# A mixture-of-experts stage on one core: experts ordered by a rough choice, buffers freed in pairs, weight halves loaded first, the last unit in two PSUM banks

## The chip, the core and the metric

One core of a Trainium2 chip runs the whole program. Its engines are TensorE (PE in the profile, with PEld for its weight loads), VectorE (DVE), ScalarE (ACT), GpSimd (POOL) and the sync engine (SP), which here issues the loads from HBM. The metric is the time of one execution on the device, in microseconds.

## The reference

Input `x` is 128 tokens of width 512. Three residual blocks follow one another: a cross-attention to 12,544 context tokens, a self-attention with 16 heads of width 128, and a mixture of experts. Only the third is touched by the change; this is what it computes (`x` there is the layernorm of the running sum, n = 128):

```
logits = x @ gate_w.T;  scores = sigmoid(logits);  sc = scores + gate_bias      # 32 experts
group_scores = sum of the two largest sc in each of 4 groups of 8 experts
gidx = the 2 best groups;  tmp = where(group chosen, sc, 0)
topk_idx = the 4 largest of tmp;  topk_w = scores[topk_idx] / their sum * 2
y   = sum over chosen experts of topk_w * ( silu(x @ w1[e]) * (x @ w3[e]) ) @ w2[e]   # 512 -> 256 -> 512
out = y + ( silu(x @ shared_gate) * (x @ shared_up) ) @ shared_down                   # 512 -> 512 -> 512
```

Ties in either choice go to the lower index.

## The kernel before

The two attention blocks take about the first 960 us of the profiled execution and are the same in both kernels. The expert block then runs as follows (all in `fast_block`; every tensor is fp32, so each matmul of the program is two instructions in the trace).

**Gating.** A layernorm, four transposes and one small product give the scores `sc` (DVE, through the helper `vec`, L1996: every small DVE step of this block has that line). The exact choice follows in fifteen dependent DVE steps: it ranks the groups with ties resolved (`gt`, `eq`, `rank`, `gsel`), masks the scores (`kept_`), takes the eight largest (`t8`), and selects the top four with ties resolved (`over_`, `n_over`, `equal`, `run`, `sel`). The helper `pin` keeps instructions in the order in which the code writes them.

**Order of the experts.** Experts 0 to 5 are "fixed": their weights are loaded during the self-attention and every token is put through them. The other 26 are sorted by how many tokens chose them. `sort_experts` counts with two small matmuls (`counts`, L2151 and L2152, from `sel`), then makes sort keys, each expert's place and the one-hot matrix `hot` on DVE. `find_loads` turns this into expert numbers with one matmul (`index`, L2169) and a DVE step; SP reads the numbers into registers and then issues the loads (`load_piece`, L1850). `gates` computes the gate values from `sel`.

**Units.** Fifteen units follow each other in the order `ffffnffntnwwntn`: `f` is a fixed expert; `t` one of the two most-chosen experts, put to all 128 tokens; `w` two experts of up to 64 tokens each; `n` four experts of up to 32 tokens each. The experts of one `w` or `n` unit are its lanes: they use separate columns of TensorE side by side. A unit has four steps. `unit_up` (L2075) multiplies by w1 and w3 in four chunks of 128 rows, all lanes of a chunk before the next chunk. `unit_act` computes silu(gate part) * up part on ACT and DVE. `unit_turn` (L2102) transposes on TensorE. `unit_down` multiplies by w2 (L2116 `y` for `w` and `n` units, L2062 `acc` for the others). For `w` and `n` units `unit_combine` (L2062) adds the rows back to their tokens. The main loop is software-pipelined: turn of unit u, up of u+1, combine of u-1, down of u.

**Loads.** Each of the 26 sorted experts comes in three pieces of 512 KB: piece 0 holds chunks 0 and 1 of w1 and w3, piece 1 holds chunks 2 and 3, piece 2 holds w2. That makes 78 loads, issued by SP in one fixed order. Before, a unit's pieces come as lane 0 piece 0, lane 0 piece 1, lane 1 piece 0, and so on, and then all pieces 2. A piece goes to the first buffer in a list `free`. `release` puts the buffers of a unit back after its up and after its down step; the load that takes a buffer waits until TensorE has read it. In program order each load also waits for the load eight before it.

**Shared expert.** Its six 512 KB buffers are filled during the self-attention. It runs inside the loop at units 5 (`shared_gate`), 6 (`shared_up`, then `check_sums`, whose small matmul `n_far`, L2315, waits for a DVE chain), 7 (`shared_turn`) and 11 (`shared_down`). All six buffers go back to `free` after `shared_down`.

Of the kernel before, what the change touches and what calls it, by code (L numbers as in the profile page):

```python
# [10 lines left out]
AF = mybir.ActivationFunctionType  # L11
ALU = mybir.AluOpType
# [758 lines left out]
def fast_block(ctx: ExitStack, tc: tile.TileContext, a: dict, out: bass.AP, amiss: bass.AP):  # L771
# [115 lines left out]
    def row(tag, name, shape=(P, D)):  # L887
        return xc.tile(list(shape), FP, tag=tag, name=name)
# [1044 lines left out]
    shared, shared_parts = {}, []  # L1933
    for nm, where in (
        ("shared_gate", homes[6][:2]),
        ("shared_up", [homes[6][2], homes[7][0]]),
        ("shared_down", homes[7][1:]),
    ):
        shared[nm] = [where[c // 2][:, c % 2 * D : c % 2 * D + D] for c in range(NC)]
        shared_parts += where  # L1940
# [34 lines left out]
    loads = []  # L1975
    for kind, lanes, _ in units:
        if kind != "all":
            loads += [(i, k) for i, _, _ in lanes for k in range(2)] + [(i, 2) for i, _, _ in lanes]

    h3 = rowp.tile([P, D], FP, tag="h", name="h3")  # L1980
    layernorm(h3, x2, "x2", pin)
    warm = spare("warm_h3")
# [23 lines left out]
    gs = row("gs", "gs", (P, G))  # L2006
    vec("tensor_tensor", gs, m8[:, :, 0], m8[:, :, 1], ALU.add)


    other = gs.unsqueeze(1).to_broadcast([P, G, G])  # L2010
    own = gs.unsqueeze(2).to_broadcast([P, G, G])
    gt = row("gt", "gt", (P, G, G))
    vec("tensor_tensor", gt, other, own, ALU.is_gt)
    eq = row("eq", "eq", (P, G, G))
    vec("tensor_tensor", eq, other, own, ALU.is_equal)
    vec("tensor_tensor", eq, eq, before, ALU.mult)
    vec("tensor_tensor", gt, gt, eq, ALU.add)
    rank = row("rank", "rank", (P, G))
    vec("tensor_reduce", rank, gt, AX.X, ALU.add)
    gsel = row("gsel", "gsel", (P, G))  # L2020
    vec("tensor_scalar", gsel, rank, float(TG), None, ALU.is_lt)
    kept_ = row("kept_", "kept_", (P, E))
    vec(
        "tensor_tensor",
        kept_.rearrange("p (g e) -> p g e", g=G),
        sc.rearrange("p (g e) -> p g e", g=G),
        gsel.unsqueeze(2).to_broadcast([P, G, E // G]),
        ALU.mult,
    )

    t8 = row("t8", "t8", (P, 8))
    vec("max", t8, kept_)
    bound = t8[:, TOPK - 1 : TOPK]
    over_ = row("over_", "over_", (P, E))
    vec("tensor_scalar", over_, kept_, bound, None, ALU.is_gt)
    n_over = row("n_over", "n_over", (P, 1))
    vec("tensor_reduce", n_over, over_, AX.X, ALU.add)
    equal = row("equal", "equal", (P, E))  # L2040
    vec("tensor_scalar", equal, kept_, bound, None, ALU.is_equal)
    run = row("run", "run", (P, E))
    vec("tensor_tensor_scan", run, ones[:, :E], equal, 0.0, ALU.mult, ALU.add)
    sel = row("sel", "sel", (P, E))
    vec("tensor_scalar", sel, run, n_over, float(TOPK), ALU.add, ALU.is_le)
    vec("tensor_tensor", sel, sel, equal, ALU.mult)
    vec("tensor_tensor", sel, sel, over_, ALU.add)


    acc = ps_o.tile([P, D], FP, tag="o", name="acc")  # L2050
# [76 lines left out]
    def unit_combine(u):  # L2127
        if units[u][0] == "some":
            k = units[u][2]
            add_to_acc(back[:, k * P : (k + 1) * P], outs[u % 2], u == len(units) - 1)  # L2130

    index_of = {}

    def release(u, pieces):
# [12 lines left out]
    def sort_experts():  # L2147

        n = SORTED
        ct = bank("counts", (P, 128))  # L2150
        pin(nc.tensor.matmul(ct[:n, :n], lhsT=ones[:, :n], rhs=sel[:, FIXED:], start=True, stop=True))  # L2151
        pin(nc.tensor.matmul(ct[:n, n : n + 1], lhsT=sel[:, FIXED:], rhs=ones[:, 0:1], start=True, stop=True))  # L2152

        keys = row("keys", "keys", (P, SORTED + 1))
        vec("scalar_tensor_tensor", keys[:n, :n], ct[:n, :n], float(E), nat[:n, :n], ALU.mult, ALU.subtract)
        vec("scalar_tensor_tensor", keys[:n, n:], ct[:n, n : n + 1], float(E), nat_col[:n], ALU.mult, ALU.subtract)
        more = row("more", "more", (P, SORTED))
        vec("tensor_scalar", more[:n], keys[:n, :n], keys[:n, n:], None, ALU.is_gt)
        place = row("place", "place", (P, 1))
        vec("tensor_reduce", place[:n], more[:n], AX.X, ALU.add)  # L2160
        vec("tensor_scalar", place[:n], place[:n], 1.0, None, ALU.add)
        hot = row("hot", "hot", (P, SORTED))
        vec("tensor_scalar", hot[:n], nat[:n, :n], place[:n], None, ALU.is_equal)
        return hot[:n]

    def find_loads(hot):
        n = SORTED
        ix = bank("index", (P, 128))
        pin(nc.tensor.matmul(ix[0:1, :n], lhsT=nat_col[:n], rhs=hot, start=True, stop=True))  # L2169
        index = small.tile([1, SORTED], mybir.dt.int32, tag="index", name="index")  # L2170
        vec("tensor_scalar", index, ix[0:1, :n], float(FIXED - 1), float(E - 1), ALU.add, ALU.min)
        order = []
# [20 lines left out]
            load_more()  # L2193

    def gates():
        vec("tensor_tensor", gate, sel, prob, ALU.mult)
        wsum = row("wsum", "wsum", (P, 1))
        vec("tensor_reduce", wsum, gate, AX.X, ALU.add)
        vec("tensor_scalar", wsum, wsum, 1e-20, None, ALU.add)
        winv = row("winv", "winv", (P, 1))  # L2200
        vec("reciprocal", winv, wsum)
        vec("tensor_scalar", gate, gate, winv, ROUTE_SCALE, ALU.mult, ALU.mult)
# [125 lines left out]
    sorted_gates_b(hot)  # L2328
# [20 lines left out]
    for u in range(3, n):  # L2349
# [19 lines left out]
    pin(nc.sync.dma_start(out=out, in_=res))  # L2369
# [80 lines left out]
```

## Time and profile before

| | us |
|---|---|
| median of three timed runs | 1094.71 (1092.88 to 1095.63) |
| time of the profiled execution | 1091.79 |
| its span, first to last instruction | 1090.1 |
| mean granted TensorE clock | 0.997 |
| expert block, from the first unit's matmul to the last instruction of the output | 966.8 to 1084.6 |
| PE busy over the whole span | 1064.8 (98%) |

The page shares are averages over three blocks with different limits, so the answers that matter here are those cut to the time after 966 us: busy time and DMA rate by stretch, who waited for whom, the chain that ended last, and the rows in order of time. In the DMA rows the time of an issue is when SP issued it, and the landing comes later.

### The profile page before, as it was taken

The numbers are of one execution on the slowest core, as the hardware profiler recorded it, in microseconds if no ns is written. First come the engines' busy times: TensorE is split into PE (matmuls) and PEld (weight loads), VectorE is DVE, ScalarE is ACT, GpSimd is POOL, SyncE is SP. The second block draws the span as 40 slices with busy tenths as digits, with TensorE's granted clock in tenths as the row PEclk, the third lists the DMA queues.
The fourth block names the chain that finished last, engine by engine and source line by source line (L and its number), as shares of the span: only waits on it lengthen the run. The fifth ranks groups of instructions, "written<-read, shape, count | busy, mean of one in ns | idle before, by whom it ended". The sixth has DMA issues, their size and how long they took to land.

```text
span 1090.1 us, 23595 instructions
## 1 busy us (share of the span) xinstructions
PE 1064.8 (98%) x10464; PEld 844.3 (77%) x10464; DVE 545.6 (50%) x668; ACT 356.1 (33%) x438; POOL 691.0 (63%) x374
## 2 busy tenths in 40 slices
PE   8999999999999999999999999999999899999996
PEld 6778888888888888888888888888888669754332
DVE  3676864574445544455444554445544568441110
ACT  2353333333333333333333333333333324303111
POOL 2256886887878778787787888889888600000000
PEclk9999999999999999999999999999999999999999
DMA  9221021101111011110124201111010499519995
GB/s 307 90 79 41 2 88 40 41 1 40 40 40 41 2 40 40 40 41 2 40 82 165 59 2 40 40 40 40 1 41 1 141 390 368 174 72 413 384 414 234
DMA packets 43247, 113.17 MB, mean 104 GB/s; under 512 B 6720, under 2 KB 12032, under 8 KB 42112
## 3 DMA queue, kind: packets, MB, share of 16 engines
q1 hardware_dynamic: 43136, 111.57, 28.2%
q8 instruction: 84, 1.38, 0.5%
q14 instruction: 27, 0.22, 0.1%
HBM read 111.26 MB, written 0.29 MB: 102 GB/s over the span
## 4 chain that ended last, share of the span: by engine, by line
PE 89%; DVE 3%; DMA 3%; POOL 2%; ACT 1%; issue 1%; SPq 0%; DVEq 0%; ACTq 0%; POOLq 0%
PE kp L1078 27%; PE vp L1078 25%; PE sb L1162 10%; PE av_new L1268 8%; PE up L2075 4%; PE acc L2062 2%; PE ssq L1015 1%; PE qp L1759 1%; PE kp L1759 1%; PE yp L1917 1%; PE svp L1780 1%; PE vp L1230 1%; DMA h<-in_experts 1%; DMA wo<-in_experts 1%; DMA wv<-in_experts 1%; DVE p L1251 1%
## 5 line engine op out<-in xcount | busy, mean ns | idle before, releaser
L1426 POOL TENSOR_TENSOR ls<-ls,p 128x2048 f32<-128x2048 f32 x81 | 369.1, 4556 | 38.2 <-ACT p L1259 36.6
L1259 ACT ACTIVATE p<-p 128x2048 f32<-128x2048 f32 (+1 forms) x95 | 179.9, 1893 | 462.1 <-DVE p L1251 461.9
L1251 DVE SCALAR_TENSOR_TENSOR p<-sb,rinv,mb_new 128x2048 f32<-128x2048 f32 (+1 forms) x86 | 199.9, 2325 | 59.2 <-PE sb L1162 59.2
L1123 POOL TENSOR_TENSOR sq<-sq 128x512 f32<-128x512 f32 x96 | 96.2, 1002 | 33.1 <-ACT sq L1117 29.3
L1162 PE MATMUL sb<-qT_txt,kraw 32*128 32x128 f32 (+1 forms) x3040 | 111.5, 283 | 1.5 <-DVE p L1251 1.5
L1162 PEld LDWEIGHTS sb<-qT_txt,kraw 32*128 32x128 f32 (+1 forms) x3040 | 93.4, 186 | 19.6 <-issue 17.1
L1078 PE MATMUL kp<-xs,w_k_w 128*128 128x256 f32 x384 | 95.4, 392 | 0.0
L1078 PE MATMUL kp<-ctx,w_k_w 128*128 128x256 f32 x384 | 93.3, 386 | 0.0
L1078 PE MATMUL kp<-xs,kt 128*128 128x256 f32 x384 | 92.7, 385 | 0.1
L1268 PE MATMUL av_new<-p,v 128*32 128x128 f32 (+1 forms) x2720 | 92.5, 276 | 0.0
L1078 PE MATMUL vp<-vt,xs 128*128 128x256 f32 x384 | 91.1, 380 | 1.1 <-ACT kraw L1106 1.1
L1078 PE MATMUL vp<-w_v_w,xs 128*128 128x256 f32 x384 | 90.9, 380 | 0.0
L1078 PE MATMUL vp<-w_v_w,ctx 128*128 128x256 f32 x384 | 90.8, 380 | 0.0
L818 POOL TENSOR_TENSOR rinv<-ms,neghalf 128x2 f32<-128x2 f32 (+4 forms) x51 | 39.6, 778 | 71.2 <-DVE ms L1025 71.2
L1078 PEld LDWEIGHTS kp<-xs,kt 128*128 128x128 f32 x384 | 73.6, 193 | 11.4 <-POOL wk L1426 0.4
L1078 PEld LDWEIGHTS kp<-xs,w_k_w 128*128 128x128 f32 x384 | 69.3, 190 | 16.3 <-issue 8.9
L1078 PEld LDWEIGHTS vp<-vt,xs 128*128 128x128 f32 x384 | 72.8, 190 | 11.4 <-ACT kraw L1106 1.6
L1078 PEld LDWEIGHTS kp<-ctx,w_k_w 128*128 128x128 f32 x384 | 70.9, 190 | 13.7 <-issue 5.3
L1078 PEld LDWEIGHTS vp<-w_v_w,xs 128*128 128x128 f32 x384 | 72.9, 190 | 10.0
L1078 PEld LDWEIGHTS vp<-w_v_w,ctx 128*128 128x128 f32 x384 | 72.9, 190 | 9.8
L1268 PEld LDWEIGHTS av_new<-p,v 128*32 128x32 f32 (+1 forms) x2720 | 69.6, 110 | 11.2 <-issue 1.2
L818 POOL TENSOR_TENSOR rs_x<-ve_x,neghalf 128x1 f32<-128x1 f32 x3 | 1.7, 551 | 101.2 <-DVE ve_x L826 101.2
(441 smaller groups left out, 1470.4 us busy)
## 6 DMA issues: line engine op xcount, KB each, us to landing
ctx<-in_ctxT SPq DMA_DIRECT2D x23, 1024.0 KB, 4.9
wo<-in_experts SPq DMA_DIRECT2D x20, 512.0 KB, 9.9
wo<-in_wo_codes SPq DMA_DIRECT2D x8, 512.0 KB, 6.9
wq<-in_experts SPq DMA_DIRECT2D x8, 512.0 KB, 9.8
wk<-in_experts SPq DMA_DIRECT2D x8, 512.0 KB, 9.2
wv<-in_experts SPq DMA_DIRECT2D x8, 512.0 KB, 9.2
q<-in_experts SPq DMA_DIRECT2D x8, 512.0 KB, 9.4
f<-in_experts SPq DMA_DIRECT2D x8, 512.0 KB, 9.7
```

The costliest lines, as they stand in the source:

```text
L818: return nc.gpsimd.tensor_tensor(dst, src, neghalf[:m, :n], op=ALU.pow)
L1015: pin(nc.tensor.matmul(sp[:m, j : j + 1], lhsT=sq[b][:, 0, o : o + m], rhs=ones[:, 0:1], start=True, stop=True,))
L1078: pin(nc.tensor.matmul(t[:, h, :], lhsT=lhs, rhs=rhs, start=(first and h == 0 and c == 0), stop=(h == 1 and c == 1), skip_group_check=True,))
L1123: pin(nc.gpsimd.tensor_tensor(sq[b][:, :w, ks], sq[b][:, :w, ks], sq[b][:, w : 2 * w, ks], op=ALU.add))
L1162: pin(nc.tensor.matmul(s[:m, i, g * P : (g + 1) * P], lhsT=kraw[b][rows, g, o : o + m], rhs=qT[part][rows, g, :], start=True, stop=True,))
L1251: pin(nc.vector.scalar_tensor_tensor(p[:m, k : k + n], s[:m, k : k + n], rinv[:m, t : t + 1], m_bc[part][:m, k : k + n], ALU.mult, ALU.sub ...
L1259: pin(nc.scalar.activation(p[:m, k : k + n], p[:m, k : k + n], AF.Exp))
L1268: pin(nc.tensor.matmul(avp[part][i * XHD : (i + 1) * XHD, g, :], lhsT=vv[b][:m, t - tile0[b], hd * XHD : (hd + 1) * XHD], rhs=p[:m, i, g * ...
L1426: pin(nc.gpsimd.tensor_tensor(d, d, src, op=ALU.add))
L1759: pin(nc.tensor.matmul(pp[:, k, :], lhsT=w[:, c, k * SHD : (k + 1) * SHD], rhs=hT2[:, c, :], start=(c == 0), stop=(c == NC - 1),))
L2062: pin(nc.tensor.matmul(acc, lhsT=lhsT, rhs=rhs, start=(n_acc == 0), stop=last))
L2075: pin(nc.tensor.matmul(up[r : r + m, :], lhsT=lhsT, rhs=w13_of((kind != "all", i), c), start=(c == 0), stop=(c == NC - 1), skip_group_chec ...
```

## The change

1. **Rough choice.** The two best groups are found by a threshold (the second largest of four group scores, from an eight-wide maximum over the scores padded with -3e38), the scores of other groups are set to zero in the same step, and every score not below the fourth largest is marked (`rough`). This takes four DVE steps. `counts` reads `rough`. The fifteen steps of the exact choice become a generator, `choosing`: two steps are issued after the `counts` matmuls, two after the `index` matmul, the rest at the start of `gates`. A memset on POOL fills the padding ahead of the layernorm.
2. **Opening order.** Before: up of unit 0, one chunk of unit 1, sort, one chunk of unit 1, find loads, gates, two chunks of unit 1. After: three chunks of unit 0, sort, the last chunk of unit 0, find loads, gates, up of unit 1. In the sort, `place + 1` is folded into the comparison that makes `hot`.
3. **Halves first.** A unit's loads are all its pieces 0, then all pieces 1, then all pieces 2.
4. **Shared buffers by twos.** The two buffers of `shared_gate` and of `shared_up` go back to `free` as soon as each has been used.
5. **Last unit in two banks.** For the last unit the gate half and the up half (256 columns each) have a PSUM bank each, in the order gate 0, up 0, gate 1, up 1, then the combine of unit 12, then gate 2, gate 3, up 2, up 3. The sigmoid and the first product are issued after gate 3.

```diff
-            loads += [(i, k) for i, _, _ in lanes for k in range(2)] + [(i, 2) for i, _, _ in lanes]
+            loads += [(i, k) for k in range(3) for i, _, _ in lanes]
...
+    gs8 = row("gs8", "gs8", (P, 8))
+    pin(nc.gpsimd.memset(gs8, -3e38))
...
+    g8 = row("g8", "g8", (P, 8))
+    vec("max", g8, gs8)
+    rough = row("rough", "rough", (P, E))
+    vec("scalar_tensor_tensor", by_group(rough), gs.unsqueeze(2).to_broadcast([P, G, E // G]),
+        g8[:, TG - 1 : TG], by_group(sc), ALU.is_ge, ALU.mult)
     t8 = row("t8", "t8", (P, 8))
-    vec("max", t8, kept_)
+    vec("max", t8, rough)
+    vec("tensor_scalar", rough, rough, t8[:, TOPK - 1 : TOPK], None, ALU.is_ge)
...
+    def last_unit():
+        u = len(units) - 1
+        _, lanes, at_ = units[u]
+        up = [spare(f"up_{u}_{h}", (P, F)) for h in range(2)]
+        for h, c in [(0, 0), (1, 0), (0, 1), (1, 1), (0, 2), (0, 3), (1, 2), (1, 3)]:
+            if (h, c) == (0, 2):
+                unit_combine(u - 2)
+            for i, r, m in lanes:
+                pin(nc.tensor.matmul(up[h][r : r + m, :],
+                    lhsT=picked[c][:, at_ * P + r : at_ * P + r + m],
+                    rhs=w13_of((True, i), c)[:, h * F : (h + 1) * F],
+                    start=(c == 0), stop=(c == NC - 1), skip_group_check=True))
+            if (h, c) == (0, 3):
+                sig = held["sig"][:, u % 2, :]
+                pin(nc.scalar.activation(sig, up[0], AF.Sigmoid))
+                hg = held["hg"][:, u % 2, :]
+                pin(nc.vector.tensor_tensor(hg, up[0], sig, ALU.mult))
+        pin(nc.vector.tensor_tensor(hg, hg, up[1], ALU.mult))
...
-        vec("tensor_scalar", place[:n], place[:n], 1.0, None, ALU.add)
-        vec("tensor_scalar", hot[:n], nat[:n, :n], place[:n], None, ALU.is_equal)
+        vec("tensor_scalar", hot[:n], nat[:n, :n], -1.0, place[:n], ALU.add, ALU.is_equal)
...
     def gates():
+        for _ in choosing:
+            pass
...
         vec("tensor_tensor", ssig, ssig, sp[nm], ALU.mult)
+        free.extend(shared_parts[nm])
+        load_more()
...
-        free.extend(shared_parts)
+        free.extend(shared_parts["shared_down"])
...
-    unit_up(0)
-    unit_up(1, [0])
+    unit_up(0, [0, 1, 2])
     hot = sort_experts()
-    unit_up(1, [1])
+    unit_up(0, [3])
     find_loads(hot)
     gates()
-    unit_up(1, [2, 3])
+    unit_up(1)
     sorted_gates_a()
...
-        if u + 1 < n:
+        if u + 1 < n - 1:
             unit_up(u + 1)
             unit_act(u + 1)
-        unit_combine(u - 1)
+        elif u + 1 < n:
+            last_unit()
+        if u != n - 2:
+            unit_combine(u - 1)
         unit_down(u)
```

More of the change, by code (lines that the diff above doesn't have):

```diff
@@ L1932, in fast_block @@
     ao_halves = halves(ao.rearrange("p j b i -> p j (b i)"))
-    shared, shared_parts = {}, []
+    shared, shared_parts = {}, {}
     for nm, where in (
@@ L1939, in fast_block @@
         shared[nm] = [where[c // 2][:, c % 2 * D : c % 2 * D + D] for c in range(NC)]
-        shared_parts += where
+        shared_parts[nm] = where
         for h, t in enumerate(where):
@@ L2005, in fast_block @@
         vec("max", m8[:, g, :], sc[:, g * (E // G) : (g + 1) * (E // G)])
-    gs = row("gs", "gs", (P, G))
+    gs = gs8[:, :G]
     vec("tensor_tensor", gs, m8[:, :, 0], m8[:, :, 1], ALU.add)
[L2010 to L2022, printed above, removed]
-    vec(
[L2024 to L2027, printed above, removed]
+    by_group = lambda t: t.rearrange("p (g e) -> p g e", g=G)
+    g8 = row("g8", "g8", (P, 8))
+    vec("max", g8, gs8)
+    rough = row("rough", "rough", (P, E))
+    vec(
+        "scalar_tensor_tensor",
+        by_group(rough),
+        gs.unsqueeze(2).to_broadcast([P, G, E // G]),
+        g8[:, TG - 1 : TG],
+        by_group(sc),
+        ALU.is_ge,
         ALU.mult,
@@ L2033, in fast_block @@
     t8 = row("t8", "t8", (P, 8))
-    vec("max", t8, kept_)
[L2035 to L2043, printed above, removed]
@@ L2044, in fast_block, with choose @@
-    sel = row("sel", "sel", (P, E))
-    vec("tensor_scalar", sel, run, n_over, float(TOPK), ALU.add, ALU.is_le)
-    vec("tensor_tensor", sel, sel, equal, ALU.mult)
-    vec("tensor_tensor", sel, sel, over_, ALU.add)
+    vec("max", t8, rough)
+    vec("tensor_scalar", rough, rough, t8[:, TOPK - 1 : TOPK], None, ALU.is_ge)
+    sel = row("sel", "sel", (P, E))
+    def choose():
+        other = gs.unsqueeze(1).to_broadcast([P, G, G])
+        own = gs.unsqueeze(2).to_broadcast([P, G, G])
+        gt = row("gt", "gt", (P, G, G))
+        yield vec("tensor_tensor", gt, other, own, ALU.is_gt)
+        eq = row("eq", "eq", (P, G, G))
+        yield vec("tensor_tensor", eq, other, own, ALU.is_equal)
+        yield vec("tensor_tensor", eq, eq, before, ALU.mult)
+        yield vec("tensor_tensor", gt, gt, eq, ALU.add)
+        rank = row("rank", "rank", (P, G))
+        yield vec("tensor_reduce", rank, gt, AX.X, ALU.add)
+        kept_ = row("kept_", "kept_", (P, E))
+        gsel = row("gsel", "gsel", (P, G))
+        yield vec("tensor_scalar", gsel, rank, float(TG), None, ALU.is_lt)
+        yield vec(
+            "tensor_tensor",
+            by_group(kept_),
+            by_group(sc),
+            gsel.unsqueeze(2).to_broadcast([P, G, E // G]),
+            ALU.mult,
+        )
+        k8 = row("k8", "k8", (P, 8))
+        yield vec("max", k8, kept_)
+        bound = k8[:, TOPK - 1 : TOPK]
+        over_ = row("over_", "over_", (P, E))
+        yield vec("tensor_scalar", over_, kept_, bound, None, ALU.is_gt)
+        n_over = row("n_over", "n_over", (P, 1))
+        equal = row("equal", "equal", (P, E))
+        yield vec("tensor_scalar", equal, kept_, bound, None, ALU.is_equal)
+        yield vec("tensor_reduce", n_over, over_, AX.X, ALU.add)
+        run = row("run", "run", (P, E))
+        yield vec("tensor_tensor_scan", run, ones[:, :E], equal, 0.0, ALU.mult, ALU.add)
+        yield vec("tensor_scalar", sel, run, n_over, float(TOPK), ALU.add, ALU.is_le)
+        yield vec("tensor_tensor", sel, sel, equal, ALU.mult)
+        yield vec("tensor_tensor", sel, sel, over_, ALU.add)
@@ L2050, in fast_block @@
+    choosing = choose()
     acc = ps_o.tile([P, D], FP, tag="o", name="acc")
@@ L2130, in unit_combine @@
             add_to_acc(back[:, k * P : (k + 1) * P], outs[u % 2], u == len(units) - 1)
+    def last_unit():
[6 more added lines that the diff above has]
+            for i, r, m in lanes:
+                pin(nc.tensor.matmul(
+                    up[h][r : r + m, :],
+                    lhsT=picked[c][:, at_ * P + r : at_ * P + r + m],
+                    rhs=w13_of((True, i), c)[:, h * F : (h + 1) * F],
+                    start=(c == 0),
+                    stop=(c == NC - 1),
+                    skip_group_check=True,
+                ))
+            if (h, c) == (0, 3):
[4 more added lines that the diff above has]
+        pin(nc.vector.tensor_tensor(hg, hg, up[1], ALU.mult))
     index_of = {}
@@ L2150, in sort_experts @@
         ct = bank("counts", (P, 128))
-        pin(nc.tensor.matmul(ct[:n, :n], lhsT=ones[:, :n], rhs=sel[:, FIXED:], start=True, stop=True))
-        pin(nc.tensor.matmul(ct[:n, n : n + 1], lhsT=sel[:, FIXED:], rhs=ones[:, 0:1], start=True, stop=True))
+        pin(nc.tensor.matmul(ct[:n, :n], lhsT=ones[:, :n], rhs=rough[:, FIXED:], start=True, stop=True))
+        pin(nc.tensor.matmul(ct[:n, n : n + 1], lhsT=rough[:, FIXED:], rhs=ones[:, 0:1], start=True, stop=True))
+        next(choosing)
+        next(choosing)
         keys = row("keys", "keys", (P, SORTED + 1))
@@ L2169, in find_loads @@
         pin(nc.tensor.matmul(ix[0:1, :n], lhsT=nat_col[:n], rhs=hot, start=True, stop=True))
+        next(choosing)
+        next(choosing)
         index = small.tile([1, SORTED], mybir.dt.int32, tag="index", name="index")
```

## Prediction

> **What bounds the kernel now.** I read four answers on the expert block, in this order: busy time by stretch, the waits of TensorE, the chain that ended last, and the rows at the two ends. Busy time by stretch:
>
> ```profile
> core 0: us, PE busy (x) PEld busy (x) DVE busy (x) ACT busy (x) POOL busy (x), PEclk, DMA share, GB/s
> 975.00:1016.00 41.00, 41.00 (x150) 18.20 (x149) 9.46 (x22) 10.95 (x26) 0.00 (x0) 1.00 1.00 401
> 1016.00:1030.00 14.00, 12.13 (x61) 4.97 (x60) 2.63 (x12) 1.71 (x4) 0.00 (x0) 1.00 0.94 354
> 1030.00:1070.00 40.00, 40.00 (x207) 12.86 (x205) 5.18 (x12) 6.31 (x16) 0.00 (x0) 1.00 1.03 413
> ```
>
> Two resources are full at once. DMA is at 1.00 and 1.03 except around 1016 to 1030, and PE is busy without a break except there. So whatever shortens one of them is soon met by the other. The waits of PE after 966 us (line that waited, what ended it, us in total, times, longest) say how much the loads cost it:
>
> ```profile
> PE n_far L2315 <- DVE far L1996: 1.9, 1, 1.9
> PE up L2075 <- DMA wo<-in_experts: 1.5, 1, 1.5
> ...
> PE y L2116 <- ACT moe_ht L2103: 0.5, 1, 0.5
> ```
>
> Only one wait is for a load, and the chain (start, us, what) shows that it is the last unit's:
>
> ```profile
> 1072.95 3.62 PE up L2075 x26
> 1076.57 2.77 PE acc L2062 x6
> 1079.34 0.23 PE hgt L2102 x2
> ...
> 1080.08 1.97 PE y L2116 x16
> ```
>
> The rows put the first matmuls of this last up step at 1069.98, where three of its four lanes could run. The fourth lane's weights landed at 1072.90, so the real loss is 1072.95 - 1069.98 = 2.97 us. Everything before 1069.98 is PE's own work. That number caps the gain: if every load were there at once, the end would come about 3 us earlier and no more. The hole in the DMA stream is in SP's issues:
>
> ```profile
> 1016.65 0.33 SPq L1850 DMA_DIRECT2D l<-in_experts  x1
> 1024.07 0.33 SPq L1850 DMA_DIRECT2D wk<-in_experts  x1
> 1025.79 0.87 SPq L1850 DMA_DIRECT2D q<-in_experts  x2
> ```
>
> SP had no free buffer for 7.4 us, until unit 7's up step read one. Loads land 1.27 us apart when the stream is full (512 KB at 413 GB/s). The landing of the `q` load came 2.66 us after the one before it, so this hole costs 1.4 us of stream.
>
> **The change, part by part.** All sums are against the profiled execution: span 1090.1, its time 1091.79. The median of the timed runs, 1094.71, is 2.92 above that. I carry a difference over to the median unchanged.
>
> *Opening.* The rows of PE and of DVE before:
>
> ```profile
> 971.25 0.23 PE L2151 MATMUL counts<-sel,ones 128*26 128x26 f32 x2
> ...
> 972.85 0.20 PE L2169 MATMUL index<-hot,nat_col 26*1 26x26 f32 x2 [0.27 <-DVE hot L1996]
> ```
> ```profile
> 968.74 0.17 DVE L1996 TENSOR_REDUCE rank<-gt 128x4 f32<-128x16 f32 x1
> ...
> 971.01 0.19 DVE L1996 TENSOR_TENSOR sel<-sel,over__7613 128x32 f32<-128x32 f32 x1
> ...
> 974.00 0.24 DVE L1996 TENSOR_SCALAR gate<-gate,winv 128x32 f32<-128x32 f32 x1
> ```
>
> The four rough steps start at 968.03, where `gt` did. By their nearest rows they take 0.17, 0.24, 0.20 and 0.24 us plus 0.035 us of handover each: `rough` at 968.98 instead of 971.20. But `counts` now stands behind three chunks of unit 0 instead of five. Six matmuls 0.43 us apart from 966.76 free PE at 969.42. So PE, not DVE, releases `counts`, 1.83 us earlier. The folded `place` step takes off another 0.18. The two exact steps put behind `counts` run before PE has finished it. The two behind `index` end at about 971.1, when `index` reaches DVE, and cost 0 to 0.1. First load: 974.59 - 2.0 = 972.6.
>
> The price is at the gates. Eleven exact steps (968.74 to 971.20, 2.46 us) and the gate steps (973.19 to 974.24, 1.05) now stand behind the `index` step, which moves to 971.1. They end at 974.5 to 974.8. PE needs the gates once `index` (970.84 to 971.04) and unit 1's four chunks are through, at about 974.5, against 974.80 for `gate_tp` before. So PE passes this point 0 to 0.3 us earlier; I take 0.1. If the cover of unit 1 were gone, the whole 3.5 us would stand on PE. The memset runs on POOL, which has no work in the last two stretches above; it stands ahead of the layernorm's one POOL step (963.22), and I price it at nothing.
>
> *Shared buffers and halves.* Two buffers come back at 1010.6 and two at 1020.3 instead of all six at 1056.7. That fills the gap in issues, so the 1.4 us hole goes. The last load lands at 1079.14 - 2.0 - 1.4 = 1075.7. The order by halves changes no byte; it lets the last unit's chunks 0 and 1 start when its fourth piece has landed, not its seventh. With the stream 3.4 us ahead, the fourth piece lands about 1065.8 and the eighth at 1074.16 - 3.4 = 1070.8.
>
> *Last unit.* PE reaches it at 1069.98 - 0.1 = 1069.9, all pieces 0 there. Twice as many matmuls of half the width: four side by side take 0.43 us at 512 columns and, in the cross-attention's `av_new` rows, 32 of 128 columns take 1.01 us, which is 0.13 per four, so about 0.25 per four at 256 columns is an upper bound and 0.22 the proportional value. I take proportional: the same 3.57 us as an `n` unit's up. The combine in its middle adds two changes between narrow and full-width matmuls. Such a change shows 0.11 us (an up step's last slot ends at 1037.38, the next `acc` starts at 1037.49), so 0.2. Then 2.77 for the combine and the down of unit 13, 0.23 for the transpose, 0.5 for ACT's copy. `y` starts at 1069.9 + 3.57 + 0.2 + 2.77 + 0.23 + 0.5 = 1077.2 instead of 1080.08. Its weights have been there since 1075.7, so PE sets the end. The gate sigmoid and products (0.38, 0.42, 0.42) lie under gate 3 to the down of unit 13 and gain nothing, since the copy waits for the transpose, and that stands behind `acc` in PE's order. After `y` nothing changes.
>
> The Trainium skill's page "TensorEngine Tiling (Array Packing)" speaks against this part. Its section Instruction Overhead gives each matmul about 60 cycles of overhead, whatever its width, and its section Key Properties says that a change of tiling mode drains TensorE. The 32 extra matmuls at 60 cycles of 2.4 GHz would be 0.8 us (an estimate from that page and the clock in "Trainium Kernel Development and Optimization", NeuronCore Architecture), and the gain would be 2.1 instead of 2.9.
>
> Sum: 1080.08 - 1077.2 = 2.9 us. 1094.71 - 2.9 = 1091.8 us, 0.27% faster. What a measurement of this kernel can tell from no change is about 0.3%, 3.3 us; the forecast lies just inside it.
>
> **The rivals.** *Loads were slower in the timed runs (faster, by more than 0.3%).* The timed runs are 2.9 us above the profiled one, and nothing shown says where. If it is the stream, the old kernel pays all of it, and the new one has 1077.2 - 1075.7 = 1.5 us of cover. The gain is then up to 2.9 + 1.5 = 4.4: 1090.3. Against it: 98% of the span is PE's, so the excess may lie in the blocks before.
>
> *Part of the cover is lost (same).* Gates late by the whole 0.3 to 1 us, the upper price of the narrow matmuls (64 in 16 fours at 0.25 is 4.0, so 0.5 more), or a small new hole. The gain is 1 to 2.4: 1092.3 to 1093.7.
>
> *The stream outruns its buffers (slower).* The loads start 2 us earlier, but PE, which empties the buffers, does not. In order behind one waiting issue stand all later loads, and PE waits for those. For it: SP already waited 12.3 us on `up` in seven places. Against it: most of those waits end while six or more loads are in flight. Each hole of the kind seen costs 1.4 us. One is covered; from the fourth on the end is later than before (1075.7 + 5.6 = 1081.3, against 1080.08), and six put `y` at 1084.1, 4.0 us later: 1098.7.
>
> *The rough choice does less than it says (same).* It takes 2.2 us off DVE's chain and PE keeps 0.4 of that. If the first load did not move at all, the filled hole alone would bring the last landing to 1079.14 - 1.4 = 1077.7 and the eighth piece to 1072.8, before PE wants chunk 2 (1069.9 + 1.8 + 1.1 = 1072.8). Then `y` starts on the landing, at 1077.8: a gain of 2.3, 1092.4 us.
>
> **How the numbers follow.** The forecast case, PE path with a gain of 2.4 to 3.6, has 0.50; a scatter of some tenths puts 0.17 of it over 3.3 us. Slower loads in the timed runs 0.27, of which 0.26 over the bound. Lost cover 0.10, a start that does not move 0.04. Outrun buffers 0.09, of which 0.07 beyond 0.3% on the slow side. Faster 0.43, same 0.50, slower 0.07. The range runs from 1089.3 (4.4 of gain and 1.0 of the 2.75 us that the timed runs spread) to 1094.0 (1 us of gain and 0.3 of the spread).
>
> **What would show it.** Right: first load at about 972.6; no gap of 7 us in SP's issues; last landing near 1075.7; no wait of an up step for a load; n_far's 1.9 us unchanged; `y` near 1077.2, on PE's path. Wrong: PE waiting for loads in a middle unit (outrun buffers), `gate_tp` after 975 (gates late), the last up step over 4 us (narrow matmuls), or `y` released by a landing.

## The result, and the profile after

| | before | after |
|---|---|---|
| median of the timed runs | 1094.78 us (7 runs, 1092.88 to 1095.63) | 1090.57 us (7 runs, 1089.49 to 1092.74) |
| time of the profiled execution | 1091.79 us | 1092.74 us |
| its span | 1090.1 us | 1091.0 us |
| end of the `gate_ps` matmul, where the expert block begins | 966.93 us | 970.49 us |
| last `y` step begins, counted from there | +113.15 us | +110.51 us |

The ratio of the timed runs is 0.9967, with a 95% interval of 0.9955 to 0.9978: faster by 4.2 us, 0.33%. The two profiled executions say the opposite, the changed one being 0.95 us longer. The last two rows of the table resolve this. Up to `gate_ps` both kernels compute the same but for one memset on POOL, and there the changed one happened to be 3.56 us later; behind that point it is 2.64 us shorter. So everything below is counted from the end of `gate_ps`, written with a plus sign, and the 3.56 us are taken up at the end.

First the opening, in PE's rows in order of time (start, duration, engine, line, operation). The first row gives the zero point, 969.77 + 0.72 = 970.49:

```profile
969.77 0.72 PE L1992 MATMUL gate_ps<-gw,hT 128*128 128x32 f32 x5
...
973.08 0.23 PE L2200 MATMUL counts<-rough,ones 128*26 128x26 f32 x2
...
974.49 0.20 PE L2219 MATMUL index<-hot,nat_col 26*1 26x26 f32 x2
...
978.32 0.27 PE L2263 MATMUL gate_tp<-ident,gate 128*26 128x128 f32 x1
```

`counts` is at +2.59 (before +4.32), `index` at +4.00 (before +5.92), `gate_tp` at +7.83 (before +7.87). So the sort is 1.9 us earlier and the gates are no later. Which of parts 1 and 2 (the rough choice, the opening order) brings how much of this is not shown: no run has one without the other. SP's issues show both ends of the stream's first half, the first load and the place where the hole was:

```profile
976.25 0.95 SPq L1850 DMA_DIRECT2D bv<-in_experts  x2
...
1021.38 0.33 SPq L1850 DMA_DIRECT2D l<-in_experts  x1
1022.66 1.60 SPq L1850 DMA_DIRECT2D n<-in_experts  x2
1027.59 0.33 SPq L1850 DMA_DIRECT2D wk<-in_experts  x1
```

The first load is issued at +5.76 instead of +7.66. The second of the two `n` loads is issued by 1024.26, and the silence up to the next load is 3.3 us, where before it was 7.1 (1016.98 to 1024.07). The loads in flight cover it: no landing there is late. Busy time by stretch, the three stretches of before moved by 3.5 us:

```profile
core 0: us, PE busy (x) PEld busy (x) DVE busy (x) ACT busy (x) POOL busy (x), PEclk, DMA share, GB/s
978.50:1019.50 41.00, 41.00 (x149) 18.18 (x149) 9.47 (x22) 10.95 (x26) 0.00 (x0) 1.00 1.02 406
1019.50:1033.50 14.00, 12.13 (x61) 4.96 (x60) 2.63 (x12) 1.71 (x4) 0.00 (x0) 1.00 1.03 416
1033.50:1073.50 40.00, 40.00 (x206) 12.83 (x204) 5.19 (x12) 6.29 (x16) 0.00 (x0) 1.00 1.03 414
```

The middle stretch moves 416 GB/s instead of 354. PE is as busy as it was, because the 1.87 us that it still misses there are `n_far`'s. PE's waits behind `gate_ps`:

```profile
PE n_far L2371 <- DVE far L1998: 1.9, 1, 1.9
PE acc L2087 <- ACT moe_att_img L2149: 0.8, 1, 0.8
PE y L2141 <- ACT moe_ht L2128: 0.5, 1, 0.5
```

No wait for a load is left. And the chain that ended last (start, us, what) no longer contains a DMA:

```profile
1073.20 0.37 PE hgt L2127 x2
1073.57 1.86 PE up L2166 x32
1075.43 1.05 PE acc L2087 x2
1076.48 1.86 PE up L2166 x32
1078.35 1.91 PE acc L2087 x4
1080.26 0.23 PE hgt L2127 x2
...
1080.57 0.38 ACT moe_ht L2128
1080.95 0.04 issue
1081.00 1.97 PE y L2141 x16
```

The chain now runs on PE from one unit to the next. The last unit's loads landed at 1080.44 (+109.95), 0.56 us before `y` began.

### The profile page after: what moved, and what is told of

It is laid out like the page before. It is cut to its first block, busy times and chain, and to the rows that moved or that the text cites. A ratio compares the mean times of both kernels' runs of the same rounds, so it can differ in the third digit from the quotient of the medians.

```text
span 1091.0 us, 23664 instructions
## 1 busy us (share of the span) xinstructions
PE 1066.1 (98%) x10496; PEld 845.1 (77%) x10496; DVE 546.1 (50%) x671; ACT 356.1 (33%) x438; POOL 691.3 (63%) x375
## 4 chain that ended last, share of the span: by engine, by line
PE 92%; DVE 3%; POOL 2%; ACT 1%; issue 1%; DMA 0%; SPq 0%; DVEq 0%; ACTq 0%; POOLq 0%
PE kp L1078 27%; PE vp L1078 25%; PE sb L1162 10%; PE av_new L1268 8%; PE up L2100 4%; PE acc L2087 2%; PE ssq L1015 1%; PE qp L1759 1%; PE kp L1759 1%; PE yp L1917 1%; PE svp L1780 1%; PE y L2141 1%; PE vp L1230 1%; DVE p L1251 1%; PE kp L994 1%
```

## The experiments

The theory under test (A): the loads held PE up for 2.97 us at the last unit, the early return of four shared buffers brings them forward, and from there PE's own work sets the end. The rivals: the opening carries the gain, or the last two parts do, or loads remain the bound. The numbers of all runs, with the end of `gate_ps` in the profiled execution, the last landing and the last `y` counted from it, and the ratio of the timed runs to those of before in the same comparison:

| kernel | parts of the change | `gate_ps` ends | last landing | last `y` | ratio (95%) |
|---|---|---|---|---|---|
| before | none | 966.93 | +112.21 | +113.15 | |
| after | 1 to 5 | 970.49 | +109.95 | +110.51 | 0.9967 (0.9955 to 0.9978) |
| e1 | 1, 2 | 968.68 | +112.35 | +113.26 | 0.9993 (0.9984 to 1.0003) |
| e2 | 4 | 967.26 | +110.10 | +110.94 | 0.9969 (0.9959 to 0.9980) |
| e3 | 1, 2, 4 | 967.16 | +108.51 | +110.15 | 0.9960 (0.9946 to 0.9973) |
| e4 | 3, 5 | 968.86 | +112.52 | +112.17 | 0.9984 (0.9975 to 0.9993) |
| e5 | none, half loads | 967.10 | +91.71 | +110.20 | 0.9958 (0.9944 to 0.9971) |
| e6 | 1 to 5, half loads | 969.84 | +87.96 | +110.50 | 0.9970 (0.9959 to 0.9982) |
| e7 | 1 to 4, `n_far` later | 968.81 | +109.81 | +110.23 | 0.9957 (0.9944 to 0.9971) |
| e8 | none, again | 968.60 | +112.32 | +113.25 | one run |
| e9 | 1 to 4 | 967.25 | +108.47 | +110.14 | 0.9966 (0.9952 to 0.9979) |
| e10 | 1 to 5, `n_far` later | 971.20 | +108.64 | +108.87 | 0.9957 (0.9943 to 0.9970) |
| e11 | 1 to 5, again | 970.00 | +108.82 | +110.50 | 0.9970 (0.9959 to 0.9981) |
| e12 | 1, 2, 4, `n_far` later | 970.12 | +109.10 | +109.91 | 0.9959 (0.9945 to 0.9972) |

The ratios are uncertain by about 1.3 us either way and can't order the variants, beyond setting e1, and in part e4, apart from the rest. The last `y` repeats to 0.1 us for the same kernel (before +113.15 and +113.25, after +110.51 and +110.50), so it is what tells them apart.

**e1_opening: the rough choice and the opening order alone.** Parts 1 and 2 of the change, with the order of a unit's loads, the return of the buffers and the last unit as before. On the kernel before; the edits of the rough choice are those of part 1 and are not printed again (`sort_experts` counts from `rough`, and `gates` begins with the rest of `choosing`):

```diff
-    unit_up(0)
-    unit_up(1, [0])
+    unit_up(0, [0, 1, 2])
     hot = sort_experts()
-    unit_up(1, [1])
+    unit_up(0, [3])
     find_loads(hot)
     gates()
-    unit_up(1, [2, 3])
+    unit_up(1)
```

> The old kernel with parts 1 and 2 alone: the rough choice and the new opening order. Old order of loads, all six shared buffers back after shared_down, last unit in one bank. Measure inside the block: from the end of gate_ps to the start of the last unit's y it was 113.15 us in the old kernel's profile and 110.51 in the new one's. Theory A (PE and the load stream take turns; an early start is worth something only if buffers are there): the first load comes 2.0 us earlier after the end of gate_ps, but the issue that waited for unit 7's up step (1024.07 in the old profile) cannot move, since PE sets it. The stream runs empty 2 us earlier, the hole grows from 1.4 to about 3.4 us, and every later landing is where it was. The block is 113.15, at most 0.3 shorter; timed, within 0.05% of the old kernel. Rival B (parts add up, each by what it takes from the loads): 2.0 us shorter, 111.1, timed 0.18% faster.

Measured: nothing gained, +113.26. The loads start 1.9 us earlier, and meet the same missing buffers. SP's issues around unit 7:

```profile
1018.32 0.33 SPq L1850 DMA_DIRECT2D l<-in_experts  x1
1025.77 0.33 SPq L1850 DMA_DIRECT2D wk<-in_experts  x1
```

The 7.45 us from issue to issue are as before (7.42), because the gap ends when unit 7's up step has read a buffer, and that is PE's time. But the stream now runs dry sooner: three landings there came 3.01, 3.04 and 1.47 us apart, 3.7 us more than three full-rate steps of 1.27, where in the kernel before the one late landing had shown 1.4. The last landing is where it was. An earlier start is given back in full as long as the buffers don't come earlier.

**e2_shared: the early return alone.** On the kernel before:

```diff
-    shared, shared_parts = {}, []
+    shared, shared_parts = {}, {}
...
-        shared_parts += where
+        shared_parts[nm] = where
...
         vec("tensor_tensor", ssig, ssig, sp[nm], ALU.mult)
+        free.extend(shared_parts[nm])
+        load_more()
...
-        free.extend(shared_parts)
+        free.extend(shared_parts["shared_down"])
```

> The old kernel with part 4 alone: shared_gate's and shared_up's buffers go back as soon as each is used. Theory A: no gap of 7 us in the issues, the hole of 1.4 us in the landings is gone, the last landing comes 1.4 us earlier (100.9 us after the first landing in the old profile, about 99.5 here), the last up step's fourth lane starts 1.4 earlier, block 111.75, timed 0.13% faster. If the load stream did not set the end (rival: PE alone), nothing changes: 113.15.

Measured: +110.94, where 111.75 was expected: 2.2 us sooner than before, against 2.6 for the whole change, from two times two buffers that come back early. The 77 steps from first to last landing took 98.82 us instead of 100.91, so the early return was worth 2.1 us of stream, not 1.4. Part of the difference is a second late landing in the stream of before, twelve places behind the hole: 1.65 us after the one ahead of it (1.71 in e8, 1.62 in e1), 1.25 in e2. The chain that ended last:

```profile
1070.39 4.31 PE up L2075 x32
1074.70 2.77 PE acc L2062 x6
```

The last up step takes 4.31 us instead of 3.57: its fourth lane starts 0.75 us behind the others, at 1071.08, on a load that landed at 1071.03 (a first matmul of the step, and the first row that takes in the late lane):

```profile
1070.32 0.62 PE L2075 MATMUL up<-l,aoT 128*32 128x512 f32 x1
...
1071.08 0.72 PE L2075 MATMUL up<-l,aoT 128*32 128x512 f32 x2
```

So here the loads still cost 0.74 us, and no wait of PE shows it, since the other lanes keep it busy.

**e3_opening_shared: the opening and the early return.** The edits of e1 and e2 together; the order of a unit's loads and the last unit stay as before.

> Parts 1, 2 and 4 together, with the old order of loads and the last unit in one bank. Theory A: the two need each other. Loads 3.4 us earlier in all, the last unit's up step no longer waits for a load, and PE sets the end: 1069.9 + 3.57 + 2.77 + 0.23 + 0.5 = 1077.0 by the old profile's clock times, block 110.1, which is 3.1 shorter and some 0.3 shorter than with the last unit in two banks. Timed 0.28% faster. Rival B (parts 3 and 5 carry a share of the gain): 0.5 to 1 us longer than the full change, 111.0 to 111.5.

Measured: +110.15. With the buffers there, the opening's earlier start does reach the end: the last landing moves from +110.10 to +108.51, and the 0.74 us of e2's up step go (it takes 3.57). The two parts are not a sum: 0 and 2.2 alone, 3.0 together.

**e4_halves_last: the order by halves and the two banks alone.** Parts 3 and 5 on the kernel before, with `last_unit` as in the change:

```diff
-            loads += [(i, k) for i, _, _ in lanes for k in range(2)] + [(i, 2) for i, _, _ in lanes]
+            loads += [(i, k) for k in range(3) for i, _, _ in lanes]
...
-        if u + 1 < n:
+        if u + 1 < n - 1:
             unit_up(u + 1)
             unit_act(u + 1)
-        unit_combine(u - 1)
+        elif u + 1 < n:
+            last_unit()
+        if u != n - 2:
+            unit_combine(u - 1)
```

> The old kernel with parts 3 and 5 alone: halves first, last unit in two banks. Theory A: the loads' times do not move. The last unit's pieces 0 have all landed about 1069.0, so its first half runs at 1070, its second waits for the eighth piece at 1074.2 and ends at 1076.1, but y then waits for the last landing at 1079.1. Block 112.3, 0.9 shorter, with y released by a landing and not by ACT's copy. Timed 0.08% faster. If narrow matmuls cost their upper price, the up step has 0.5 us more, still hidden by the landing: the same block.

Measured: `y` begins at +112.17, 1.0 us sooner, but the final sum ends only 0.64 us sooner. PE's longest wait for a load shows one reason:

```profile
PE up L2141 <- DMA wo<-in_experts: 0.7, 1, 0.7
```

The chain that ended last shows the other, at its end:

```profile
1066.31 10.12 DMA wo<-in_experts
1076.42 0.04 issue
1076.47 1.91 PE up L2141 x26
...
1081.03 2.31 PE y L2116 x16
```

PE can start on the halves that are there. Two lanes reach chunk 2 at 1074.84, the last one 1.63 us later on the eighth piece, and 0.65 us of that show as a wait. And the `y` step does not wait for the last landing as expected: it is released by ACT's copy, begins before its last weights have landed, and takes 2.31 us instead of 1.97. The parts help when the loads are late, by hiding some of the lateness.

**e5_before_half and e6_after_half: PE's floor.** The same edit in both kernels; only half of the columns of each sorted expert's piece is loaded, and all of the matmuls stay. The other half of each buffer holds whatever was there before:

```diff
-        pin(nc.sync.dma_start(out=t, in_=src))
+        if index is None:
+            pin(nc.sync.dma_start(out=t, in_=src))
+        else:
+            pin(nc.sync.dma_start(out=t[:, :512], in_=a["experts"][bass.ds(index, 1), :, k * 1024 : k * 1024 + 512].rearrange("e p f -> (e p) f")))
```

> The old kernel with each of the 78 sorted loads cut to the first half of its columns (256 KB instead of 512), so that half of each expert's weights are whatever the buffer held. Same issues, same waits for buffers, same work on every engine; the load stream has twice the room. Theory A: only the wait of the last up step goes, 2.97 us: block (end of gate_ps to the start of the last y) 110.2, the last up step without a wait. Timed: if the stream costs the old kernel in the timed runs what it does in its profile, 3.0 us faster, ratio 0.9973. Rival C (the stream is slower in timed runs than in that one profile): 4 us or more, ratio 0.9963 or less.

> The new kernel with the same cut of its 78 loads. Theory A: the new kernel is set by PE, so its block stays 110.5 within 0.1, and its time is that of the new kernel, ratio 0.9967 to the old one within 0.0010. It is also slower than the cut old kernel by the price of the two banks, 0.3 us, which the times can hardly tell. Rival C: if the stream still sets the new kernel's end in some runs, it gets up to 1 us faster than the new kernel, ratio 0.9958.

Measured: +110.20 for the kernel before, which is 2.95 us sooner, and +110.50 for the changed one, which is nothing. The third of the stretches, in the kernel before with half loads:

```profile
1030.00:1070.00 40.00, 40.00 (x205) 12.92 (x203) 5.18 (x12) 6.15 (x16) 0.00 (x0) 1.00 0.66 231
```

The same stretch in the changed kernel with half loads:

```profile
1032.90:1072.90 40.00, 40.00 (x208) 12.83 (x211) 5.19 (x12) 6.37 (x16) 0.00 (x0) 1.00 0.58 201
```

With DMA at about half of its rate PE is as full as before. Inside the block this settles the mechanism: the 2.97 us of late loads were all that there was to gain, and the changed kernel has taken them. It also shows that the changed kernel's floor lies 0.3 us above that of the old one. The timed runs agree for the changed kernel (0.9970 with half loads and, in e11, with whole ones) but not for the kernel before: 0.9958 is 4.8 us, where theory A had 3.0 (0.9973, outside the interval) and the rival 4 or more. That is taken up with the rivals below.

**e9_onebank: the change without the two banks.** On the changed kernel:

```diff
-        if u + 1 < n - 1:
+        if u + 1 < n:
             unit_up(u + 1)
             unit_act(u + 1)
-        elif u + 1 < n:
-            last_unit()
-        if u != n - 2:
-            unit_combine(u - 1)
+        unit_combine(u - 1)
```

> The change without its part 5: the last unit in one PSUM bank again, with the combine of the unit before behind it; parts 1 to 4 stay. All numbers count from the end of the gate_ps matmul. Theory A (TensorE sets the end; the second bank costs it time and gives none): the last y at +110.15, as in the run with parts 1, 2 and 4, against +110.51 in the changed kernel; no load wait of an up step over 0.2 us; the small gaps inside the two-bank step (0.36 us in sum) gone. Timed within 0.1% of the changed kernel's ratio, 0.996 to 0.997. Rival B (the stream still sets part of the end and the second bank hides it): with the last landing at about +110 as in the changed kernel, the up step waits for its seventh or eighth piece, some 0.3 to 0.6 us, and the y is at +110.5 to +110.8.

Measured: +110.14, equal to e3. So part 3 changes nothing in this position and part 5 costs 0.36 us. The rival was not put to the test, since the last landing came at +108.47 and not at about +110. The chain:

```profile
1070.31 3.57 PE up L2100 x32
1073.88 2.77 PE acc L2087 x6
1076.65 0.23 PE hgt L2127 x2
```

Against these 3.57 + 2.77 = 6.34 us stand 1.86 + 1.05 + 1.86 + 1.91 = 6.68 with two banks: 0.15 for the narrow matmuls, 0.19 for the combine in the middle of the up step.

**e7, e10 and e12: PE's next wait taken away.** `n_far` is 1.87 us of PE's floor. In three variants its matmul stands behind the shared expert's transposes, where its data are ready. On the changed kernel (e10; e7 is the same with one bank, e12 without parts 3 and 5):

```diff
-        n_far = bank("n_far")
+        return far
+
+    def count_far(far):
+        n_far = bank("n_far")
         pin(nc.tensor.matmul(n_far[0:1, 0:1], lhsT=far, rhs=ones[:, 0:1], start=True, stop=True))
...
-            check_sums()
+            far = check_sums()
...
             shared_turn()
+            count_far(far)
```

> A version meant to be better: the new kernel with the last unit in one bank again, and with the n_far matmul and the step that reads it issued one unit later, behind shared_turn, so that PE does not wait 1.9 us for the DVE chain. Theory A: PE's floor falls by 1.87 + 0.3, to 108.3 for the start of the last y. Then the last landing decides (108.5 to 110 after gate_ps in the runs so far), and y's last lane waits for it. From gate_ps to the end of the final sum: 113.0 to 114.0 against 115.04 in the new kernel. Timed ratio to the old kernel 0.9950 to 0.9957. Rival: if PE's wait for n_far is filled elsewhere (another wait for DVE takes its place), 114.7 as in the run with parts 1, 2 and 4.

> The whole change, and the n_far matmul with the step behind it moved from ahead of the shared expert's transposes to behind them, so that TensorE no longer waits 1.87 us for the VectorE chain; the last unit stays in two banks. Counted from the end of gate_ps. Theory A (TensorE is the floor of the changed kernel, and with n_far's wait gone the loads are next): TensorE's own path is 110.51 - 1.87 = +108.64, the last landing in the runs so far lies between +108.5 and +110.0, so the last y starts on a landing or just behind it, +108.7 to +110.0, with the order by halves and the two banks now worth some tenths against the one-bank run of the same move (+110.23). Rival C (the stream follows TensorE, because buffers come back only when TensorE has read them): the landings move with TensorE by the 1.87 us, the last one to +108.1, and y at +108.64 on TensorE's path. Timed: 0.9950 to 0.9965 by A, 0.995 or less by C.

> Parts 1, 2 and 4 of the change (opening and the early return of the shared buffers; old order of a unit's loads, last unit in one bank), and the n_far matmul moved behind the shared expert's transposes. Counted from the end of gate_ps. TensorE's path would be 110.15 - 1.87 = +108.3. Theory A (loads are next): with the landings of the run with parts 1, 2 and 4 (last at +108.5) the last weights of the up step land 6.2 us ahead of the last landing, at +102.3, and y follows 7.2 us behind that, at +109.5; an up wait for a load of 1.2 us. Rival C (the stream follows TensorE): y at +108.3 and no load wait. Timed 0.995 to 0.996 by A, 0.994 to 0.995 by C.

Measured: with one bank (e7) `y` came at +110.23, a miss: 0.3 us sooner than in the changed kernel, and no sooner than in e9, which differs from it by the move alone. The final sum ended at +114.77, the 114.7 of the rival, but not by the rival's cause: the wait was gone, and no other wait for DVE took its place. Three single gaps in the landings (2.97, 2.09 and 1.98 us; e9's stream has one, of 2.80) had put the last one at +109.81, and the chain begins with a load again:

```profile
1063.61 9.97 DMA m<-in_experts
1073.58 0.04 issue
1073.63 1.91 PE up L2100 x10
```

With two banks (e10) and a smoother stream, +108.87: 1.64 us sooner than the changed kernel (the wait was 1.87), 4.28 sooner than before, and the earliest of all. The rows of PE show where the rest went: the up step behind the old place of `n_far` starts 1.96 us sooner, the one behind its new place 1.73, the next `y` 1.63. Its two later stretches:

```profile
1020.20:1034.20 14.00, 14.00 (x64) 5.55 (x62) 2.63 (x12) 1.71 (x4) 0.00 (x0) 1.00 1.03 414
1034.20:1074.20 40.00, 40.00 (x233) 13.30 (x232) 5.19 (x12) 6.97 (x17) 0.00 (x0) 1.00 1.03 413
```

Both resources are full to the end. Without parts 3 and 5 (e12) the loads are the bound, as theory A had it. PE came to the last unit at 1071.48 and ran three lanes; the fourth lane's weights landed at 1072.85, which cost 1.42 us (1.2 expected), of which only 0.36 show as a wait:

```profile
1071.48 0.62 PE L2100 MATMUL up<-l,aoT 128*32 128x512 f32 x1
...
1072.90 0.62 PE L2100 MATMUL up<-l,aoT 128*32 128x512 f32 x2 [0.36 <-DMA l<-in_experts]
```

`y` followed 7.2 us behind that landing, as expected, at +109.91 (+109.5 was expected; the landing came 0.4 us later than assumed). The chain:

```profile
1062.88 9.97 DMA l<-in_experts
...
1072.90 3.62 PE up L2100 x26
...
1080.03 1.97 PE y L2141 x16
```

Rival C (the stream follows PE) had the landings 1.9 us earlier. They are not: the last one is at +108.64 to +109.81 without the wait and at +108.47 to +109.95 with it. Without the wait PE catches up with the loads. The last landings of e7, e10 and e12 differ by up to 1.2 us, and nothing here shows why, so how much of the 1.04 us between e10 and e12 is due to parts 3 and 5 is not settled. e10's timed ratio of 0.9957 beats the kernel before; that it beats the changed kernel (0.9970 in the same comparison) the timed runs do not show, as the intervals overlap; the block does.

**e8_before_again and e11_after_again: each kernel once more.**

> The old kernel once more, for a second profile of it. The time up to the end of gate_ps was 966.9 us in its first profile and 967.2 to 970.5 in the five others, whose code up to there is the same but for a memset. Theory A: the first profile was a lucky one in that stretch, and here it is 967 to 969.5, while the block is 113.2 within 0.3. Rival C: the block is 114 or more here, with more gaps in the landings.

> The changed kernel once more, unchanged. Theory (the blocks ahead of gate_ps scatter in levels by the half-clock stretches of TensorE near 854 to 886 us, whatever the kernel): gate_ps ends at one of the levels 967, 968.7 or 970 in the profiled execution, and what follows is the same to 0.1 us: last y at +110.5, no load wait. Rival: the changed kernel itself slows the blocks ahead of gate_ps (its profile had 970.5, the profile of before 966.9); then gate_ps ends at 970 again. Timed ratio 0.9965 to 0.9975.

Measured: the blocks repeat to 0.1 us; the end of `gate_ps` does not, and not as the theory alone would have it. Before ended it at 968.60 instead of 966.93; after at 970.00, close to its 970.49, which is what the rival said. But the timed runs of e11 fall into two groups, five from 1090.79 to 1090.96 and two at 1092.00 and 1092.11, and the profiled execution is the 1092.11. So most runs of the changed kernel were 1.2 us shorter than the one that was seen.

## Why the prediction was right, point by point

**The time.** 1091.8 was predicted, with 1089.3 to 1094.0 around it; 1090.57 was measured. The forecast case, PE's own path, is what the trace shows; the time came out faster by 0.33%, just past the 0.3% where the prediction drew its bound. Its path accounts for 2.64 of the 4.2 us, the gain of the block. The range held the other 1.5 us only because the rival of slow loads, with up to 4.4 us, was in it, and no run shows that rival at work: that the median stayed inside owes something to luck.

**The opening.** Predicted `counts` 1.83 us earlier, released by PE: 1.73. First load at 972.6 on the old clock, which is +5.67: +5.76. The eleven deferred steps at no price to the gates: `gate_tp` 0.04 earlier where 0.1 was taken. The cover, unit 1's four chunks, held.

**The hole.** Right in kind and too small. It was read from one landing gap as 1.4 us; e2, which fills only the hole, ended its stream 2.1 us sooner. The single gap did not count the late landing twelve places on, and in e8 the gap itself was 2.96 us and not 2.66.

**The last landing and the cover.** Predicted +108.8, 1.5 us ahead of `y`. The profile had +109.95, 0.56 ahead, with one gap of 2.09 us at a landing 6 places from the end; the second profile of the same kernel had +108.82 and 1.7 us of cover. The sum was right for a stream without such a gap, but a gap of this size came or did not come from run to run. One more of them (0.8 us over the full-rate step) would have used up the 0.56 us that were left. This was the weakest step.

**The last unit.** Reached at +103.0 as predicted (1073.50 - 970.49 = 103.01). `y` was predicted at +110.3 and came at +110.51: the two changes between narrow and full-width matmuls took 0.19 (0.2 predicted), and the term that was mis-sized is the one taken as proportional, 64 half-width matmuls at 3.57 us. They took 3.72. The overhead from the Trainium skill's page "TensorEngine Tiling (Array Packing)", Instruction Overhead, which would have made it 0.8 us more, does not add up over the lanes: the 32 extra matmuls cost 0.15 us in all. They are 8 extra sets of four side by side, and 60 cycles for each set would be 0.2 us (an estimate from that page and the prediction's 2.4 GHz).

**The gain of 2.9.** The block gained 2.64 in the two first profiles and 2.75 in the second two. By e5 the cap was 2.95, and the two banks gave 0.3 of it back.

**The rivals.** Outrun buffers: e1 is that rival in miniature, since its stream ran dry sooner by what it had started earlier, but in the change the returned buffers prevent it. That the loads were slower in the timed runs stays open. The second profile of before (e8), at 1093.64 a typical time, speaks against it: its excess was ahead of `gate_ps` (1.67 us) and only 0.10 behind. But half loads made the timed runs of before 4.8 us faster, 1.9 more than the block, as this rival would have it. Another reading is the place where `gate_ps` ends: e5's profiled execution, 1089.01, ended it at 967.10, among the earliest; three of its other four timed runs are within 0.2 us of that time; and none of the 11 runs of before in the same comparison comes within 0.8 us of 1091.79, the time of before with such an early `gate_ps`. Late loads in those 11 runs or later ends of `gate_ps` would both give this, and they have no trace. That the choice does less than it says, or that the gates come late, is refuted by the opening's rows and by the unmoved `gate_tp`.

**The other 1.5 us of the measured 4.2.** The excess of 2.9 us of the timed runs over the first profile, which the prediction left open, lies ahead of the expert block in the one typical execution that was traced (e8). The first profile of before was an unusually short one: `gate_ps` at 966.93, and a time below all of the timed runs. The end of `gate_ps` falls into levels, and the granted clock shows what goes with them (PEclk is its mean over the stretch). Busy time by stretch of before:

```profile
853.50:858.00 4.50, 3.91 (x16) 2.71 (x12) 3.06 (x4) 1.22 (x2) 3.66 (x2) 0.62 0.11 44
883.00:890.50 7.50, 6.85 (x37) 4.39 (x36) 4.67 (x13) 0.33 (x2) 0.55 (x1) 1.00 1.02 418
```

The same of before in its second profile, e8:

```profile
858.00:863.00 5.00, 4.52 (x44) 3.15 (x44) 1.30 (x4) 2.53 (x2) 1.75 (x1) 0.66 0.01 3
883.00:890.50 7.50, 6.05 (x26) 3.43 (x27) 5.71 (x15) 0.33 (x2) 0.00 (x0) 1.00 0.94 352
```

And of after, in its first profile:

```profile
858.00:863.00 5.00, 3.98 (x24) 2.79 (x28) 1.27 (x4) 1.91 (x1) 2.30 (x1) 0.66 0.01 3
883.00:890.50 7.50, 5.82 (x13) 2.04 (x10) 4.66 (x12) 0.00 (x0) 0.00 (x0) 0.77 0.98 367
```

Each shortfall is worth the same 1.7 us of full clock: 0.38 x 4.5, 0.34 x 5.0, 0.23 x 7.5. With one such stretch at 854 us `gate_ps` ended at 966.9 to 967.3 (before, e2, e3, e5, e9); with one at 859 or 885 at 968.6 to 968.9 (e1, e4, e7, e8); with two at 969.8 to 971.2 (after, e6, e10, e11, e12). Level by level, before at 968.60 took 1093.64, and after's five shorter runs of e11, 1.2 us below an execution that ended `gate_ps` at 970.00, took 1090.9: a difference of 2.7, which is the block's. (Those five have no trace, so their level is inferred; their mean granted clock, 0.997 against 0.995 for the two longer ones, agrees with one stretch in place of two.) What is beyond that in the first comparison may then be which levels its runs fell on; this is argued and not shown, and late loads in the timed runs are the other candidate. The median of before was 1094.78, 1094.09, 1093.84 and 1093.95 in the four comparisons.

**What stays open.** What decides on which level a run falls. All five executions with two half-clock stretches had the new opening, five of nine, against none of five without it. The code ahead of `gate_ps` is the same but for a memset on POOL, and e3 and e9, with the same memset, were at the lowest level; so nothing here shows a cause, and fourteen profiles are too few to call it chance. The Trainium skill's page "TensorE: Matmul & The Clock Gate", section What's actually happening, has the clock fall to half after an idle window, and has windows of 3413 ns that run freely and do not restart with the kernel. The stretches' length of 3.41 us agrees. That PE is idle for a whole window is not what stands right ahead of the falls: in the 3.4 us before them it was busy for 1.87 us (before, from 850.8), 1.12 (e8, from 856.2) and 1.72 (after, from 883.1). What decides on a fall is not shown by these runs.

## What to carry to other kernels

Where a stream of loads and an engine are both full, ask first which buffer is late, not which load starts late: an earlier start alone was worth nothing (e1), four buffers returned some tens of microseconds sooner were worth 2.2 us, and only then did the earlier start add its 0.8. Halving the loads in one run (e5) gives the cap of all such work beforehand, and tells whether a late-load remedy such as the split last unit (0.36 us as a price here, 0.64 us as a gain in e4, where the loads were late) is still needed. When several lanes run side by side, compare the first matmul of the step with the first one of the late lane: the wait that the profile put down to PE was 1.5 of 2.97 us before, 0.36 of 1.42 in e12, and nothing of 0.74 in e2. Compare profiles from a common point inside the span, ahead of the change: the first traces of before and after differed by 3.56 us in front of that point, more than the 2.64 that the change was worth behind it, and two traces of one kernel still by 1.67.

## What the runs showed of the hardware

- TensorE's granted clock falls to 0.5 for stretches of 3.41 us, which begin here at one or two of three places ahead of the expert block (near 854, 859 and 885 us), and each takes away 1.7 us of full clock. The one at 854 let `gate_ps` end 1.7 us sooner than one at 859 or 885, though its loss by the clock is the same.
- A full stream of 512 KB loads on one core ran at 413 to 416 GB/s, 1.27 us apart, but single landings came 1.5 to 3 us after the one ahead with five to seven other loads in flight: one to three among the first nine in every run with whole loads, the others at places that differ between kernels and runs. In the two profiles of the changed kernel the last landing differs by 1.1 us.
- Sets of four 256-column fp32 matmuls side by side took 0.23 us each (3.72 for 16 sets), against 0.22 for half of a 512-column set; the change between narrow and full-width matmuls took 0.1 us each way.
